# Attention beside a gated low-rank layer: the first block's order, the row tiles' slots and the second output pass's weight splits

## The chip, the cores and the metric

The kernel runs on one core of one Trainium2 chip. The metric is device time in microseconds (us). Matrix products run on TensorE (PE in the profile, with its weight loads as PEld), elementwise work on VectorE (DVE), ScalarE (ACT) and GpSimd (POOL). Transfers are issued from the queues of SyncE (SP) and of ScalarE.

## The reference

```
xn  = (x - mean) / sqrt(var + 1e-5)               # over 2048 columns, 4096 rows
q, k, v = split(xn @ Wqkv + bqkv)                 # 512 columns each
att = softmax(q @ k.T / sqrt(512)) @ v            # two sequences of 2048 rows
s   = (xn @ Wq.T) @ keys.T                        # 64 experts
g   = softmax over the 16 largest of s, 0 elsewhere
z   = (xn @ A.T) * repeat(g, 8)                   # 512 columns
y   = x + att @ Wo + bo + 2 * (z @ B.T)
```

All is fp32, with x of 2 x 2048 x 2048.

## The kernel before, in words

**Products.** Every fp32 operand is split into a high part, rounded to the format `fp32r` that TensorE takes (`split_hi`, ScalarE, L123), and the rest (`split_lo`, L126, VectorE). `product` and `multiply` issue three matmuls for one product of 128 x 128 by 128 x N: low by high, high by low, high by high (L131, and L1184 in the output stage).

**Order.** The program is written out in Python, and a scheduler orders the instructions of each engine by readiness under its own model of time, earlier code first; it also sets the semaphores. `behind(keys)` keeps the instructions of a block after the one last recorded under a key, on the same engine; it makes no engine wait for another. Rings (`Ring`, L42) hand out named slots of SBUF in turn, and a new user of a slot waits for the last one. Each engine works through its queue in order, so an instruction that waits holds up what stands behind it.

**Stages.** The 4096 rows form eight blocks of 512 rows.

1. `first_block` makes block 0 ready and computes its value columns. Four tiles of 128 rows (`rows`) are loaded from `x` (`load`), their mean and variance taken (`normal`: L196, L199, L344, L189, and POOL's power at L190), scaled (`scale`: three quarters on VectorE at L352, one on ScalarE at L356 and L357), and turned by TensorE into 16 chunks of 128 columns (`turn`, L366); each turned chunk is split into `xh`. The weights of the value columns come in eight pieces for each of two halves (`piece`, through `wv_piece` and `weights`: load at L266, splits at L123 and L126; loaded tiles `ws` have four slots, split ones `wh` eight). `mul` multiplies one group of 128 rows (one tile turned) by one piece: six matmuls of 264 columns. A group of the first half has 48 of them. `values_out` takes the sums out to `vs` and to memory.
2. Other columns of blocks 0 and 1 (`ftile`), and then blocks 2 to 7 in pairs, by sums and differences of half matrices in seven steps in place of eight (`phase`). Meanwhile the row statistics of the blocks to come are taken: `stats_steps` loads row tiles `xs` by ScalarE's queue (L214) and runs them through `row_stats` (L196). Blocks 1 to 3 take tiles of 1024 columns from three slots (`r_xs`), blocks 4 to 7 tiles of 512 columns from two (`r_xr`). One tile is loaded for each that is read, as many ahead as there are slots but one.
3. Attention: scores, softmax and the weighted sum of v.
4. Output: attention and the gated layer in one product of 1024 rows of weights, again in seven steps for eight (`STEPS`: P1, P2, P6, P5, P3, P7, P4). There are 16 units `q` of work: eight groups of rows in a first pass over half of the output columns, and the same eight in a second pass over the other half. A unit is seven steps, each of two products (t = 0, 1) of 12 matmuls.

**The output stage's queues.** A job is one step of one unit. `ahead(n)` prepares the row operand of job n, three jobs early: `load_x` at P1, then `stationary`, which forms the sums (L1133, L1135, L1136, L1138 on VectorE) and splits the step's operand into `s` (six slots, two for a job). P1's result is copied by ScalarE to `u` (L1196); P2 goes on in the same PSUM bank, so its products wait for that copy. The other results are added on VectorE (L1202, L1207, L1213; `finish`, L1173), with additions on POOL (L1209, L1214) into tiles `xo`, which `residual` loads and adds the bias to (L1168).

The output weights `wb` of a pass stay in SBUF, four slots to a step (`r_tm`). `moving(p, step, kk)` returns a load (L1096 or L1100, into `wo`) and a split for two of a step's four row chunks: 14 such units in a pass. In the last unit of the first pass (q = 7) and the first of the second, the loop's end loads and splits the second pass's weights: step m's load two steps ahead, its split when the first pass is done with that step, both units of a step together.

Of the kernel before, what the change touches and what calls it, by code (L numbers as in the profile page):

```python
# [20 lines left out]
ND = D // P  # L21
# [5 lines left out]
NT = T // P  # L27
# [36 lines left out]
def attn_ffn_kernel(ctx: ExitStack, tc, x, xT, wq, wv, wob, bqk, bv, bo, keysT, out):  # L64
# [24 lines left out]
    def half(*js):  # L89
        return Ring(sb, *(f"H{j}" for j in js))  # L90
# [111 lines left out]
    def stats_steps(i, r, cols, out):  # L202


        v, tiles = {}, {}
        per = C // cols

        def load(k):
            if k < NT * per:
                t, c = divmod(k, per)  # L210
                tiles[k] = r([P, cols], F32, "xs")
                r0 = i * T + t * P
                with behind("hi"):
                    nc.scalar.dma_start(tiles[k], x[r0 : r0 + P, c * cols : (c + 1) * cols])  # L214

        def rows(k):
            t, c = divmod(k, per)
            if k == 0:
                v["mv"] = const.tile([P, NT, 2], F32, name="mv", bufs=2)
                for n in range(len(r.tags) - 1):  # L220
                    load(n)
            if c == 0:
                v["st"] = const.tile([P, 4, 6], F32, name="st6", bufs=2)
                v["parts"] = 0
            load(k + len(r.tags) - 1)
# [96 lines left out]
    def first_block():  # L322
# [24 lines left out]
        def scale(t):  # L347
            for n in range(4):
                c, h = divmod(n, 2)
                v = rows[t][c][:, h * 512 : (h + 1) * 512]  # L350
                if n < 3:
                    last["row"] = nc.vector.tensor_scalar(  # L352
                        v, v, mv[:, t, 0:1], rs[:, t : t + 1], ALU.subtract, ALU.mult
                    )
                else:
                    nc.scalar.activation(v, v, AF.Identity, bias=nm[:, t : t + 1])  # L356
                    nc.scalar.mul(v, v, rs[:, t : t + 1])  # L357

        def turn(t, g0=0, g1=NCH // 4):
            sl = slice(t * P, (t + 1) * P)  # L360
# [15 lines left out]
        def piece(c2, h, eng=None, queue=None):  # L376
            return wv_piece(h, c2, eng, queue)
# [14 lines left out]
        for j in range(26):  # L392
            nc.tensor.matmul(pw, warm[:, :P], warm, start=True, stop=True)
        load(0, 512)
        wh = [piece(0, 0, None, nc.scalar)]
        normal(0)
        with behind("nm"):
            wh.append(piece(1, 0, None, nc.scalar))
        scale(0)
        load(1, 1024)  # L400
        turn(0, 0, 2)
        for c2 in range(2, 4):
            with behind("row"):
                wh.append(piece(c2, 0, None, nc.scalar))
        turn(0, 2, 4)
        ps = [acc() for t in range(NT)]
        for c2 in range(3):
            mul(ps[0], wh[c2], 0, c2)
        with behind("row"):
            normal(1)  # L410
        with behind("nm"):
            wh += [piece(c2, 0) for c2 in range(4, 6)]
        scale(1)
        load(2, 1024)
        for c2 in range(3, 6):
            mul(ps[0], wh[c2], 0, c2)
        turn(1)
        for c2 in range(6):
            mul(ps[1], wh[c2], 1, c2)
        with behind("row"):  # L420
            wh += [piece(c2, 0, nc.gpsimd) for c2 in range(6, N2)]
        load(3, 1024)
        constants()
        for c2 in range(6, N2):
            mul(ps[0], wh[c2], 0, c2)
            mul(ps[1], wh[c2], 1, c2)
            if c2 == 6:
                with behind("row"):
                    normal(2)
                scale(2)  # L430
                turn(2)
                with behind("row"):
                    normal(3)
        qr = router_in()
        for t in range(2):
            values_out(0, t, 0, r_ev, qr, ps[t])
        flush()
        for c2 in range(N2):
            mul(ps[2], wh[c2], 2, c2)
            if c2 == 2:  # L440
                scale(3)
                turn(3)
        for c2 in range(N2):
            mul(ps[3], wh[c2], 3, c2)
        for t in range(2, NT):
            values_out(0, t, 0, r_ev, qr, ps[t])
        flush()
        ps = [acc() for t in range(NT)]
# [443 lines left out]
        xn = nxt  # L892
    r_ph = wide(0, 1, 2, 3, 4, 5)
    r_pw = wide(8, 9, 7)
    r_xr = half(7, 8)
    r_xu = big(6, 7, 8)
    r_xv = wide(6)
    r_yv = mid(2, 3)
# [4 lines left out]
    n = 0  # L903
# [174 lines left out]
    def moving(p, step, kk):  # L1078


        small = p == 1 and STEPS.index(step) % 2 == 1

        def load():
            n = 2 * p
            if small:
                ws = tw[p, step, kk] = [r_wo1([P, T], F32, "wo") for k in range(2)]
            else:
                ws = tw[p, step, kk] = r_wo([P, 2, T], F32, "wo")
                ws = [ws[:, k, :] for k in range(2)] if step not in ("P1", "P2", "P3") else ws
# [24 lines left out]

        return load, split
# [7 lines left out]
            )  # L1123
            X[g, a, b] = t

    def stationary(q, step):


        g = q % (NB // 2 * NH)
# [6 lines left out]
            nc.vector.tensor_tensor(x[0, 0], X[g, "S1"], x[0, 0], ALU.subtract)  # L1136
        if step == "P3":
            nc.vector.tensor_tensor(x[0, 1], x[0, 1], x[0, 0], ALU.subtract)  # L1138
        src = {
            "P1": x[0, 0], "P2": x[0, 1], "P6": x[0, 0], "P5": X.get((g, "S1")),  # L1140
            "P3": x[0, 1], "P7": x[1, 0], "P4": x[1, 1],
        }[step]
        hi, lo = (r_s([P, ND, TH], FR, "s") for a in range(2))
        split_hi(hi, src)
        split_lo(lo, src, hi)
# [77 lines left out]
    def ahead(n):  # L1223

        if n >= len(jobs):
            return
        q, step = jobs[n]
        if step == "P1":
            load_x(q % NG) if q < 2 * NG else None
        stationary(q, step)  # L1230


    flush()
# [2 lines left out]
    for s in range(NSTEP + LAG):  # L1236
# [47 lines left out]
        if e in (2, 7, 12):  # L1284
            if e == 2:
                load_bo(0)
            with behind("mq"):
                ahead(e // 5)
    more = {}
    for q in range(2 * NG):  # L1290
        p = q // NG
        for t in range(NA):
# [2 lines left out]
        for n, step in enumerate(STEPS):  # L1295
# [7 lines left out]
            for t in range(NA):  # L1303
# [1 line left out]
                if step == "P1":  # L1305
                    bank[t] = ps
                combine(q, step, t, ps)
            if n + 3 + 7 * q >= 3:
                ahead(7 * q + n + 3)
            if q == NG - 1 and n == 0:  # L1310
                load_bo(1)


            m = n + 7 * q - 7 * (NG - 1)
            if 0 <= m < 7:
                with behind("act"):
                    for _, split in more.pop(m):
                        split()
            if -2 <= m < 5:
                more[m + 2] = [moving(1, STEPS[m + 2], kk) for kk in range(0, ND, 2)]  # L1320
                for load, _ in more[m + 2]:
                    load()


# [40 lines left out]
```

## Time and profile before

| | us |
|---|---|
| median of 3 runs | 2660.33 (2659.31 to 2663.43) |
| profiled execution, its own time | 2662.85 |
| its span in the profile | 2661.1 |
| TensorE busy | 2632.8 |
| VectorE busy | 1818.6 |
| ScalarE busy | 863.4 |
| POOL busy | 569.7 |
| granted TensorE clock, mean | 0.995 |

Busy time is that of an engine's instructions in this one execution; waits are what stood between them. In a line of a timeline the first number is the start in us from the beginning of the span, the second the duration, then engine, line, operation, output and inputs by the program's names, and in brackets the idle time before it with the instruction that ended it. In a list of waits come the total, the number of times and the longest. A slice's line gives each engine's busy time, the granted clock as a share of the full one, and what DMA moved.

### The profile page before, as it was taken

How to read it: one execution, taken by the hardware profiler on the slowest of the kernel's cores; microseconds unless marked ns; L12 is line 12 of the kernel's file. 1: busy time of each engine (PE TensorE's matmuls, PEld its weight loads, DVE VectorE, ACT ScalarE, POOL GpSimd, SP SyncE). 2: the span in 40 equal slices, each digit the busy share in tenths (PEclk: the TensorE clock that was granted, in tenths of full speed). 3: DMA queues.
4: the chain of work that ended last, by engine and by line, in shares of the span. 5: the costliest groups of instructions: out<-in, count | busy, mean ns of one | idle time of the engine just before them, and what ended most of it. 6: DMA issues, size and time to landing. Idle time of an engine off the chain costs nothing.

```text
span 2661.1 us, 33841 instructions
## 1 busy us (share of the span) xinstructions
PE 2632.8 (99%) x12881; PEld 2227.1 (84%) x12881; DVE 1818.6 (68%) x2493; ACT 863.4 (32%) x1285; POOL 569.7 (21%) x349
## 2 busy tenths in 40 slices
PE   7999999999999999999999999999999999989999
PEld 7889888888888888888888888888888888878887
DVE  6557849868878687756445676456667776796675
ACT  4223323333332333323233343334434222322221
POOL 1321420000000000000101111000012665565654
PEclk8999999999999999999999999999999999999999
DMA  6678885668546684536725476634467444655543
GB/s 232 222 259 278 297 283 178 211 212 296 186 147 225 230 291 137 173 125 221 286 101 191 143 269 229 206 111 143 144 205 260 167 162 159 201 188 165 178 155 107
DMA packets 243395, 530.42 MB, mean 199 GB/s; under 512 B 21608, under 2 KB 87200, under 8 KB 243232
## 3 DMA queue, kind: packets, MB, share of 16 engines
q1 hardware_dynamic: 229696, 497.29, 55.3%
q10 hardware_dynamic: 13536, 30.97, 3.4%
q8 instruction: 101, 1.65, 0.3%
q14 instruction: 62, 0.51, 0.1%
HBM read 393.80 MB, written 134.38 MB: 198 GB/s over the span
## 4 chain that ended last, share of the span: by engine, by line
PE 95%; DVE 2%; DMA 2%; issue 1%; ACT 0%; ACTq 0%; SPq 0%; DVEq 0%
PE acc L131 73%; PE acc L1184 22%; DMA xs<-in_x 1%; DVE wb L126 1%; DMA ws<-in_wv 0%; DVE st L196 0%; DVE pw L126 0%; PE acc L366 0%; DVE xq L666 0%; DMA wo<-tw_d 0%; DVE xo L1173 0%; PE misc L466 0%; PE misc L999 0%; DVE xh L126 0%; DVE wh L126 0%
## 5 line engine op out<-in xcount | busy, mean ns | idle before, releaser
L131 PE MATMUL acc<-t,pw 128*128 128x512 f32 x3024 | 695.6, 391 | 2.7 <-ACT t L123 1.8
L131 PEld LDWEIGHTS acc<-t,pw 128*128 128x128 f32 x3024 | 566.4, 188 | 121.3 <-ACT t L123 2.2
L1184 PE MATMUL acc<-wb,s 128*128 128x512 f32 x2688 | 611.8, 390 | 7.7 <-ACT u L1196 7.7
L1184 PEld LDWEIGHTS acc<-wb,s 128*128 128x128 f32 x2688 | 506.0, 188 | 113.4 <-ACT u L1196 8.2
L131 PE MATMUL acc<-ph,vt 128*128 128x512 f32 x1536 | 367.5, 390 | 0.0
L131 PE MATMUL acc<-qt,kt 128*128 128x512 f32 x1536 | 366.0, 389 | 0.0
L131 PEld LDWEIGHTS acc<-ph,vt 128*128 128x128 f32 x1536 | 287.4, 188 | 62.1 <-DVE ot L1047 1.2
L131 PEld LDWEIGHTS acc<-qt,kt 128*128 128x128 f32 x1536 | 288.2, 188 | 60.3 <-issue 0.2
L1168 POOL TENSOR_TENSOR xo<-xo,bo_bc 128x512 f32<-128x512 f32 x128 | 217.2, 1704 | 560.7 <-DMA xo<-in_x 330.2
L123 ACT CAST pw<-pw 128x1024 fp32r<-128x1024 f32 (+1 forms) x168 | 177.7, 1058 | 380.3 <-PE acc L131 225.0
L131 PE MATMUL acc<-xh,wh 128*128 128x512 f32 x1152 | 263.7, 390 | 0.0
L126 DVE TENSOR_TENSOR pw<-pw 128x1024 fp32r<-128x1024 f32 (+1 forms) x168 | 218.0, 1298 | 65.5 <-ACT pw L123 65.5
L131 PEld LDWEIGHTS acc<-xh,wh 128*128 128x128 f32 x1152 | 215.6, 188 | 45.0
L131 PEld LDWEIGHTS acc<-pw,t 128*128 128x128 f32 x2016 | 245.7, 188 | 1.5 <-DVE pw L126 0.2
L131 PE MATMUL acc<-pw,t 128*128 128x264 f32 x2016 | 246.5, 283 | 0.0
L123 ACT CAST s<-xz 128x1024 fp32r<-128x1024 f32 x112 | 118.1, 1054 | 384.6 <-PE acc L1184 312.9
L126 DVE TENSOR_TENSOR s<-xz,s 128x1024 fp32r<-128x1024 f32 x112 | 166.6, 1488 | 49.8 <-ACT s L123 49.8
L126 DVE TENSOR_TENSOR ph<-sp,ph 128x512 fp32r<-128x512 f32 x128 | 93.4, 732 | 120.3 <-ACT ph L123 119.5
L971 DVE TENSOR_TENSOR M<-M,sp 128x512 f32<-128x512 f32 x112 | 79.6, 711 | 123.5 <-ACT sp L965 123.1
L536 POOL TENSOR_TENSOR zt<-zt,g 128x512 f32<-128x512 f32 x24 | 35.0, 1467 | 494.8 <-DMA g<-gd 166.7
L126 DVE TENSOR_TENSOR wh<-wu,wh 128x512 fp32r<-128x512 f32 x96 | 96.1, 1025 | 64.9 <-ACT wh L123 64.9
L965 ACT COPY sp<-acc 128x512 f32<-128x512 f32 x128 | 74.8, 586 | 182.1 <-PE acc L131 182.0
(150 smaller groups left out, 2378.1 us busy)
## 6 DMA issues: line engine op xcount, KB each, us to landing
vt<-v_d SPq DMA_DIRECT2D x128, 512.0 KB, 3.5
pw<-sq_d SPq DMA_DIRECT2D x72, 512.0 KB, 3.5
xz<-oz_d SPq DMA_DIRECT2D x64, 512.0 KB, 4.2
xo<-in_x SPq DMA_DIRECT2D x128, 256.0 KB, 3.5
out_y<-xo SPq DMA_DIRECT2D x128, 256.0 KB, 2.5
pw<-in_wq SPq DMA_DIRECT2D x54, 512.0 KB, 3.9
wu<-in_wq SPq DMA_DIRECT2D x48, 512.0 KB, 7.6
xq<-in_xT SPq DMA_DIRECT2D x48, 512.0 KB, 6.1
```

The costliest lines, as they stand in the source:

```text
L123: return nc.scalar.copy(hi, src)
L126: return (eng or nc.vector).tensor_tensor(lo, src, raw(hi), ALU.subtract)
L131: last["pe"] = nc.tensor.matmul(ps, st(a_), mv(b_), start=first and n == 0, stop=end and n == 2)
L536: nc.gpsimd.tensor_tensor(zt, zt, gx[n], ALU.mult)
L965: nc.scalar.copy(st, ps)
L971: nc.vector.tensor_tensor(M[blk], M[blk], st, ALU.max)
L1168: nc.gpsimd.tensor_tensor(xs, xs, bo_bc[q // (NB // 2 * NH), c], ALU.add)
L1184: nc.tensor.matmul(ps, st[a_][:, kk, sl], mv[b_], start=not more and kk == 0 and n == 0, stop=kk == ND - 1 and n == 2, skip_group_check=more,)
```

## The change

Three places are rewritten.

In `first_block`, tile 0 is loaded, normalised and scaled first. The weights' pieces follow in groups (`pieces(n)`), all loaded by SP's queue, with splits ordered after the latest scaling of a tile (a new key, `mul`, on ScalarE's last scaling) and all on ScalarE and VectorE. The four groups are multiplied one after the other, each by all eight pieces; the next tile is normalised, scaled and turned within the loop. Before, groups 0 and 1 shared the loop over the pieces, and pieces 6 and 7 had their low part on POOL.

In `stats_steps`, row tiles are loaded ahead by the number of slots less two, and `r_xr` has a third slot, H6.

In the output stage, `stationary` is cut into `sums` and `split`; the operand of P6 is split together with that of P5, one step later, but for q = 0. The second pass's 14 weight units are handled one by one: a list `at` gives the step, counted from the start of unit 7, at which each load and split is issued, over twelve steps for the splits.

```diff
-                for n in range(len(r.tags) - 1):
+                for n in range(len(r.tags) - 2):
                     load(n)
...
-            load(k + len(r.tags) - 1)
+            load(k + len(r.tags) - 2)
...
-                    nc.scalar.mul(v, v, rs[:, t : t + 1])
+                    last["mul"] = nc.scalar.mul(v, v, rs[:, t : t + 1])
...
         load(0, 512)
-        wh = [piece(0, 0, None, nc.scalar)]
         normal(0)
-        with behind("nm"):
-            wh.append(piece(1, 0, None, nc.scalar))
         scale(0)
+        wh = []
+        def pieces(n):
+            with behind("row", "nm", "mul"):
+                while len(wh) < n:
+                    wh.append(piece(len(wh), 0))
+        turn(0, 0, 2)
+        pieces(2)
+        turn(0, 2, 4)
+        pieces(4)
         load(1, 1024)
-        turn(0, 0, 2)
-        for c2 in range(2, 4):
-            with behind("row"):
-                wh.append(piece(c2, 0, None, nc.scalar))
-        turn(0, 2, 4)
         ps = [acc() for t in range(NT)]
...
-        with behind("row"):
-            wh += [piece(c2, 0, nc.gpsimd) for c2 in range(6, N2)]
...
+        for t in range(NT):
+            if t + 1 < NT:
+                with behind("row"):
+                    normal(t + 1)
+            if t == 0:
+                pieces(6)
+                load(2, 1024)
+            for c2 in range(N2):
+                if t + 1 < NT and c2 == 2:
+                    scale(t + 1)
+                if t == 0 and c2 == 4:
+                    pieces(N2)
+                    load(3, 1024)
+                    constants()
+                if t + 1 < NT and c2 == 6:
+                    with behind("pe"):
+                        turn(t + 1)
+                mul(ps[t], wh[c2], t, c2)
...
-    r_xr = half(7, 8)
+    r_xr = half(6, 7, 8)
...
-        small = p == 1 and STEPS.index(step) % 2 == 1
+        small = p == 1 and (2 * STEPS.index(step) + kk // 2) % 4 > 1
...
-        stationary(q, step)
+        sums(q, step)
+        if step != "P6" or q == 0:
+            if step == "P5" and q:
+                split(q, "P6")
+            split(q, step)
...
-    more = {}
+    more = [moving(1, step, kk) for step in STEPS for kk in range(0, ND, 2)]
+    at = [-3, -2, -1, 0, 1, 2, 2, 3, 4, 5, 6, 7, 7, 8, 9, 10, 11]
...
-            m = n + 7 * q - 7 * (NG - 1)
-            if 0 <= m < 7:
-                with behind("act"):
-                    for _, split in more.pop(m):
-                        split()
-            if -2 <= m < 5:
-                more[m + 2] = [moving(1, STEPS[m + 2], kk) for kk in range(0, ND, 2)]
-                for load, _ in more[m + 2]:
-                    load()
+            while at and at[0] <= n + 7 * q - 7 * (NG - 1):
+                at.pop(0)
+                k = 14 - len(at)
+                if k > 0:
+                    with behind("act"):
+                        more[k - 1][1]()
+                if k < 12:
+                    more[k + 2][0]()
```

The new rule for `small` picks the same units as the old one (kk is 0 or 2), and the changed test before `load_x` always held.

More of the change, by code (lines that the diff above doesn't have):

```diff
@@ L394, in first_block @@
         load(0, 512)
-        wh = [piece(0, 0, None, nc.scalar)]
         normal(0)
-        with behind("nm"):
-            wh.append(piece(1, 0, None, nc.scalar))
         scale(0)
-        load(1, 1024)
-        turn(0, 0, 2)
-        for c2 in range(2, 4):
-            with behind("row"):
-                wh.append(piece(c2, 0, None, nc.scalar))
-        turn(0, 2, 4)
-        ps = [acc() for t in range(NT)]
-        for c2 in range(3):
-            mul(ps[0], wh[c2], 0, c2)
-        with behind("row"):
-            normal(1)
@@ L411, in first_block @@
[L411 to L420, printed above, removed]
-            wh += [piece(c2, 0, nc.gpsimd) for c2 in range(6, N2)]
[L422 to L427, printed above, removed]
-                with behind("row"):
[L429 to L433, printed above, removed]
@@ L434, in first_block @@
-        qr = router_in()
[L435 to L445, printed above, removed]
+        wh = []
[3 more added lines that the diff above has]
+                    wh.append(piece(len(wh), 0))
@@ L446, in first_block @@
+        qr = router_in()
+        for t in range(NT):
             values_out(0, t, 0, r_ev, qr, ps[t])
@@ L1124, in load_x, with sums @@
             X[g, a, b] = t
-    def stationary(q, step):
+    def sums(q, step):
         g = q % (NB // 2 * NH)
@@ L1138, in stationary, with split @@
             nc.vector.tensor_tensor(x[0, 1], x[0, 1], x[0, 0], ALU.subtract)
+    def split(q, step):
+        g = q % (NB // 2 * NH)
         src = {
-            "P1": x[0, 0], "P2": x[0, 1], "P6": x[0, 0], "P5": X.get((g, "S1")),
-            "P3": x[0, 1], "P7": x[1, 0], "P4": x[1, 1],
-        }[step]
+            "P1": (0, 0), "P2": (0, 1), "P6": (0, 0), "P3": (0, 1), "P7": (1, 0), "P4": (1, 1),
+        }.get(step)
+        src = X[(g, *src)] if src else X[g, "S1"]
         hi, lo = (r_s([P, ND, TH], FR, "s") for a in range(2))
@@ L1228, in ahead @@
         if step == "P1":
-            load_x(q % NG) if q < 2 * NG else None
-        stationary(q, step)
+            load_x(q % NG)
+        sums(q, step)
[3 more added lines that the diff above has]
+            split(q, step)
     flush()
@@ L1307, in attn_ffn_kernel @@
                 combine(q, step, t, ps)
-            if n + 3 + 7 * q >= 3:
-                ahead(7 * q + n + 3)
+            ahead(7 * q + n + 3)
             if q == NG - 1 and n == 0:
                 load_bo(1)
-            m = n + 7 * q - 7 * (NG - 1)
-            if 0 <= m < 7:
-                with behind("act"):
-                    for _, split in more.pop(m):
-                        split()
-            if -2 <= m < 5:
-                more[m + 2] = [moving(1, STEPS[m + 2], kk) for kk in range(0, ND, 2)]
-                for load, _ in more[m + 2]:
-                    load()
+            while at and at[0] <= n + 7 * q - 7 * (NG - 1):
[6 more added lines that the diff above has]
+                    more[k + 2][0]()
 def kernel(**inputs):
```

## The prediction

> **What bounds the kernel now.** I read the page's busy shares first, then everything that TensorE waited for, then each place of a long wait in order of time.
>
> ```profile
> PE 2632.8 (99%) x12881; PEld 2227.1 (84%) x12881; DVE 1818.6 (68%) x2493; ACT 863.4 (32%) x1285; POOL 569.7 (21%) x349
> ```
>
> TensorE is busy for 2632.8 of 2661.1 us, and the change keeps all matrix products. So only the 28.3 us of idle, and time at a lower clock, can be won. The waits of TensorE over the whole span (line, releaser, total, times, longest):
>
> ```profile
> PE acc L1184 <- ACT u L1196: 7.7, 1, 7.7
> PE acc L366 <- DVE xs L352: 5.1, 1, 5.1
> PE acc L131 <- DVE wh L126: 4.6, 1, 4.6
> PE acc L366 <- issue: 2.4, 1, 2.4
> PE acc L131 <- ACT t L123: 1.8, 1, 1.8
> ...
> PE acc L131 <- DVE t L126: 0.9, 1, 0.9
> PE acc L131 <- ACT wh L123: 0.5, 1, 0.5
> ```
>
> The rest is 1.2 us at the start and 4.0 us after the last product. The second, third and fourth lie in the first 50 us; the first is at 2350 us; the last three at 531 and 238 us. First the opening, from the timelines of TensorE, VectorE and ScalarE (start, duration):
>
> ```profile
> 9.72 0.63 ACT L123 CAST wh<-ws 128x528 fp32r<-128x528 f32 x1 [2.84 <-DMA ws<-in_wv]
> 12.32 0.71 DVE L126 TENSOR_TENSOR wh<-ws,wh 128x528 fp32r<-128x528 f32 x1 [1.24 <-ACT wh L123]
> 12.95 1.46 DVE L352 TENSOR_SCALAR xs<-xs,mv,rs 128x512 f32<-128x512 f32 x3
> 13.55 3.67 PE L366 MATMUL acc<-ident,xs 128*128 128x128 f32 x16 [5.13 <-DVE xs L352]
> 25.67 2.79 PE L131 MATMUL acc<-wh,xh 128*128 128x264 f32 x11 [4.64 <-DVE wh L126]
> 49.00 1.96 PE L366 MATMUL acc<-ident,xs 128*128 128x128 f32 x16 [2.36 <-issue]
> ```
>
> VectorE has the statistics of tile 0 at 7.3 us and POOL the power at 8.0, but scaling (L352) starts at 12.95: two weight subtractions stand ahead of it, and they wait for weights. The second place is the border of the output's two passes (ScalarE, VectorE, TensorE):
>
> ```profile
> 2345.19 0.58 ACT L1196 COPY u<-acc 128x512 f32<-128x512 f32 x1
> 2355.36 1.21 DVE L1136 TENSOR_TENSOR xz<-xz 128x1024 f32<-128x1024 f32 x1
> 2356.66 1.05 ACT L123 CAST s<-xz 128x1024 fp32r<-128x1024 f32 x1 [10.89 <-DVE xz L1136]
> 2357.61 0.58 ACT L1196 COPY u<-acc 128x512 f32<-128x512 f32 x1
> 2358.24 62.00 PE L1184 MATMUL acc<-wb,s 128*128 128x512 f32 x263 [7.74 <-ACT u L1196]
> ```
>
> ScalarE stands in its queue before the split of P6's operand, which waits for VectorE's sum L1136; the second `u` copy is behind it, and TensorE needs that copy. VectorE is late because it is full: its busy time is 8.69, 10.00, 10.00, 10.00 and 10.00 us in the 10 us slices from 2310 to 2360. The copies of neighbouring units start exactly 38.08 us apart; over this border (2309.74 to 2396.02, two units) it is 86.28, so it costs 86.28 - 76.16 = 10.1 us: 7.7 of idle and 2.4 of slow clock.
>
> [...] 0.50 granted from 25 to 30 us after the 4.64 us wait, 0.63 from 2350 to 2360. [...] ScalarE and VectorE run strictly in queue order; the 10.89 us above show it. [...] the 128x1024 subtraction into `s` takes 1.21 us at least and 2.24 at most.
>
> **The change, part by part.**
>
> *Opening.* The weights' eight pieces leave ScalarE's DMA queue for SP's, behind tile 0's two SP loads; their splits are ordered behind the scaling of tile 0, and no longer go to POOL (2.56 us for two there become 1.31 on VectorE). Groups 0 to 3 each run over all eight pieces in turn. In the built order TensorE has 36 products, transposes, 60, transposes, 48, transposes, 48 of group 3; before 36, 58, 50, 48. Nothing is added or taken away there, so what counts is when VectorE delivers.
> Arrival: in 1.5 us slices DMA moved 2.3 MB by 9.0 us before. Tile 0 (1.05 MB) and four pieces (4 x 0.27) are now first in the queues, 2.1 MB, so I take the fourth piece to land near 9 us (estimate; it was 15.5). On SP the four issues, 0.33 to 0.46 us each, are past at about 3.5 us; tile 1's loads follow when tile 0 has landed (4.2, as the third piece's issue did before) and are in by 11 us at 3.1 MB, wanted at 15.4: covered by 4 us. SP then issues tile 2 and half of tile 3; pieces 4 and 5 wait behind these and for a freed slot (12 us), about 4.7 MB in, which was moved at 15 us; landed by 17.
> VectorE: scaling 8.0 to 9.5. Then, from about 9.9 (ScalarE casts one piece, 0.63, then the first transposes): low parts of tile 0, 2 x 1.67 = 3.34; eight weight subtractions, 4 x 1.31 = 5.24; statistics of tile 1, 2.46; its small operations 0.43; its scaling 1.46. Sum 12.93, so the last weight piece is ready at 22.8 and pieces 4 and 5, wanted at 18.4, are there. TensorE: group 0 ends at 22.8 + 0.7 = 23.5. A group is 48 products at 0.121 us (165 in the 20 us from 240), 5.8: group 1 ends at 29.3, and 1 us for slow clock makes it 30.3. Tile 2 is scaled by then: 22.8 + low parts 3.3 + statistics 2.5 + `vs`, small ones and POOL's power 1.4 + scaling 1.5 = 31.5. Transposes end at 32.5, group 2 at 38.3. From there to group 3 the chain is the one of before (its `vs`, L344, power, scaling, transposes): 46.65 to 50.82 = 4.2 us. Group 3 starts at 42.5, with 0.3 for clock 42.8. Before 50.82: **8.0 us less**. Ends: 4 less if the clock stays low for all of group 1 (5.8 more there, 1.8 of it hidden by scaling), 11 less if there is no slow clock and the two gaps of VectorE I counted vanish.
>
> *Rows' slots.* `stats_steps` loads one row tile ahead and not two; in the last four blocks there are three slots and not two. 88 loads on ScalarE's queue stay 88. ScalarE no longer waits for VectorE to free the slot just read (up to 4.9 us at L214). This bears on the 531 us wait (2.7) and the 238 us one (0.5). I take half: **1.5 less**. Ends: 4 less (with the 0.96 clock there), 3 more if the later loads keep VectorE waiting. The cover is TensorE's lead in split weights; the rival below prices its loss.
>
> *Second pass split over twelve products.* `moving(1, ...)` is loaded and split in 14 single units over 12 products (q = 7, P1 to q = 8, P3) and not in seven pairs over seven; loads start one product earlier. The splits are the same. Their VectorE cost before was 27.6 us (all `wb` subtractions, 2312 to 2359), with 38.08 - 26.7 = 11.4 us free per unit (28 of 40 us busy elsewhere). In the built VectorE order the sums of q = 8 and its L1136 now stand ahead of the splits for P3, P7 and P4, which took 13.3 us (1.72 + 1.21 + 5.78 + 2.28 + 2.28). So L1136 falls from 2355.4 to about 2341.5, and P6's low part from 2362.1 to 2348.8; TensorE wants it at 2309.7 + 8 x 5.44 = 2353.2. ScalarE's P6 cast is then done at 2343.4, the `u` copies follow their products, and the wait is gone: **10.1 us less**. Later splits: P3's end near 2355 and are wanted at 2364; P4's near 2365, wanted at 2375. P6's split is also issued one step later in the code; in steady state the built order on ScalarE and VectorE is that of before, so I cost it at nothing. Its cover is VectorE's 4.4 us; beyond it each late us is a TensorE us. Low end of this part: 5 less.
>
> Sum: 8.0 + 1.5 + 10.1 = 19.6. Profiled execution 2662.85 (span 2661.1, 1.75 around it) becomes 2643.3; the median of the runs shown, 2660.33, becomes 2640.7, so **2641**.
>
> **Rivals.**
> - *The border's wait moves.* P6's low part or P1's split stays late, for the backlog of eight units (8 x 1.97 = 15.8 us into 9.8 free) is 6 us. For it: POOL is busy 30.5 of these 50 us and slows subtractions. Against: the order above leaves 4 us. A 4 us wait and 1 of clock: 2646.
> - *The opening gains half.* Weights land late or group 1 runs slow: [...] Then 4 less: 2645. With the first rival 2651.
> - *Slower: row tiles starve VectorE.* Between 60 and 300 us 24 tiles of 128x1024 take 5.3 us (median) to land, and one ahead may mean waiting for each. VectorE has 240 - 161.7 = 78.3 us free there. If each waits fully, 24 x 5.3 = 127 us, 49 too many: 2641 + 49 = 2690. It decides from 4.3 us per tile ((78.3 + 24.6) / 24, the bound of slower below). Against: the first of each pair is loaded a tile earlier; 12 x 5.3 = 64 us fits; today's waits there are 11.0.
>
> **How the numbers follow.** Likeliest 0.66, own range 2637 to 2645; border 0.12; opening 0.09; starved rows 0.07; other mixtures 0.06, split between no change (0.05) and slower (0.01). A difference under 0.2% (5.3 us) can't be told from none here. Faster 0.66 + 0.12 + 0.09 = 0.87, same 0.05, slower 0.08. The range runs from all favourable ends (11 + 4 + 10.1: 2635) to both small rivals together (2651), one more for run to run: 2652.
>
> **What would show it.** Right: scaling of tile 0 begins near 8 us; group 3's products near 43; no wait of TensorE at L1196's successor, copies 38.08 us apart across the border; the waits at 531 shorter. Wrong: transposes still wait over 3 us at 9; a new wait behind `s` or `wb` after 2330; idle after `xs` loads on VectorE far over today's 49.8 us in total with TensorE waiting for `wh`.

## The result, and the profile after

| | before | after |
|---|---|---|
| median of 5 runs of each, us | 2661.26 | 2643.41 (2639.48 to 2644.76) |
| ratio | | **0.9929** [0.9915, 0.9944] |
| profiled execution, its own time, us | 2662.85 | 2641.34 |
| its span, us | 2661.1 | 2639.6 |
| granted TensorE clock, mean | 0.995 | 1.000 |
| group 3's products start, us | 50.82 | 42.65 |
| from there to the second `u` copy of the first output unit, us | 1992.75 | 1989.44 |
| second `u` copies of q = 7 and q = 9 apart, us | 86.28 | 76.16 |

The prediction was 2641, its own range 2637 to 2645. The median is 17.85 us lower than before (0.67%); the means of the five are 18.8 us apart, and that is the 0.71% of the ratio. The last three rows are the places of the three edits, one after the other: 8.17 + 3.31 + 10.12 = 21.6 us, all of the 21.5 us between the two profiled executions. That this is 3.7 us more than between the medians is taken up with the clock, below. Of all executions in this document one, of `open_only`, took 11266.45 us, and its row leaves it out. Line numbers are each kernel's own: L1136 and L1196 before are L1121 and L1184 now.

The page's busy times of the changed kernel:

```profile
PE 2624.7 (99%) x12881; PEld 2220.4 (84%) x12881; DVE 1822.3 (69%) x2495; ACT 863.6 (33%) x1285; POOL 571.8 (22%) x347
```

TensorE does the same 12881 matmuls in 8.1 us less busy time. No work was taken away, so this is work done at a higher clock: the kernel before has 27.3 us with 0.50 granted up to its last product (13.65 in the opening, 3.4 at 533 us, 10.2 at the border), the changed one none. Idle time fell from 28.3 to 14.9 us, and 13.4 + 8.1 make the 21.5. Everything that TensorE waited for in the changed kernel:

```profile
PE acc L131 <- DVE wh L126: 5.0, 3, 2.2
PE acc L366 <- issue: 2.4, 1, 2.4
PE acc L131 <- DVE yv L746: 1.8, 1, 1.8
PE misc L393 <- DVE warm L390: 1.2, 1, 1.2
PE acc L131 <- ACT wh L123: 0.5, 1, 0.5
```

Gone are the wait for the `u` copy at the border (7.7 us), the one for tile 0's scaling (5.1) and both for `t` near 531 us (1.8 and 0.9). The one for `wh` at 238 us (0.5) stays, at 230 us now. The wait for weights stays at 5.0 us, but in three pieces of at most 2.2 where it was one of 4.6. One wait is new: 1.8 us behind `yv`. The opening, from the timelines of VectorE and TensorE:

```profile
8.14 1.46 DVE L352 TENSOR_SCALAR xs<-xs,mv,rs 128x512 f32<-128x512 f32 x3 [0.76 <-POOL rs L190]
...
21.42 1.32 DVE L126 TENSOR_TENSOR wh<-ws,wh 128x528 fp32r<-128x528 f32 x2
```
```profile
8.74 2.01 PE L366 MATMUL acc<-ident,xs 128*128 128x128 f32 x16
...
19.57 1.61 PE L131 MATMUL acc<-wh,xh 128*128 128x264 f32 x11 [2.22 <-DVE wh L126]
21.02 1.91 PE L366 MATMUL acc<-ident,xs 128*128 128x128 f32 x16
22.69 7.55 PE L131 MATMUL acc<-wh,xh 128*128 128x264 f32 x60
30.29 2.01 PE L366 MATMUL acc<-ident,xs 128*128 128x128 f32 x16
32.37 6.10 PE L131 MATMUL acc<-wh,xh 128*128 128x264 f32 x48
40.83 2.00 PE L366 MATMUL acc<-ident,xs 128*128 128x128 f32 x16 [2.36 <-issue]
```

Scaling starts at 8.14, as soon as POOL's power is there, and TensorE goes over to the transposes without a wait: the 26 matmuls on a constant tile at its start (L393, not changed) end there too, near 8.9. VectorE ends the eighth piece at 22.74, where the prediction had 22.8. The border (ScalarE, then VectorE):

```profile
2331.03 1.06 ACT L123 CAST s<-xz 128x1024 fp32r<-128x1024 f32 x1 [4.43 <-PE acc L1172]
...
2336.42 0.59 ACT L1184 COPY u<-acc 128x512 f32<-128x512 f32 x1 [2.08 <-PE acc L1172]
...
2374.50 0.59 ACT L1184 COPY u<-acc 128x512 f32<-128x512 f32 x1 [2.08 <-PE acc L1172]
```
```profile
2329.54 1.21 DVE L1121 TENSOR_TENSOR xz<-xz 128x1024 f32<-128x1024 f32 x1
...
2337.10 3.94 DVE L126 TENSOR_TENSOR s<-xz,s 128x1024 fp32r<-128x1024 f32 x2
```

The second copy of each unit comes 38.08 us after the last one and waits for its product. P6's cast (2331.03) still stands in front of both copies, but it no longer waits for VectorE. P6's sum (L1121, before L1136) is done at 2330.75, and its low part, the first of the two at 2337.10, near 2339.1; TensorE wants it 5.44 us after P1's last product, 2336.42 + 5.44 = 2341.9.

### The profile page after: what moved, and what is told of

Its sections match the earlier page's. It is cut to its first block, busy times and chain, and to the rows that moved or that the text cites. A ratio compares the mean times of both kernels' runs of the same rounds, so it can differ in the third digit from the quotient of the medians.

```text
span 2639.6 us, 33827 instructions
## 1 busy us (share of the span) xinstructions
PE 2624.7 (99%) x12881; PEld 2220.4 (84%) x12881; DVE 1822.3 (69%) x2495; ACT 863.6 (33%) x1285; POOL 571.8 (22%) x347
## 4 chain that ended last, share of the span: by engine, by line
PE 98%; DVE 1%; DMA 0%; ACT 0%; issue 0%; SPq 0%; ACTq 0%; DVEq 0%
PE acc L131 75%; PE acc L1172 23%; DMA xs<-in_x 0%; DVE st L196 0%; PE acc L366 0%; DVE xh L126 0%; PE misc L451 0%; PE misc L984 0%; DVE wh L126 0%; DMA v_d<-vs 0%; PE misc L1024 0%; PE misc L1025 0%; PE misc L481 0%; ACT xh L123 0%; ACT xs L357 0%
## 5 line engine op out<-in xcount | busy, mean ns | idle before, releaser
L126 DVE TENSOR_TENSOR s<-xz,s 128x1024 fp32r<-128x1024 f32 x112 | 173.2, 1548 | 42.0 <-ACT s L123 42.0
```

Of the source, the lines that this page charges most:

```text
L126: return (eng or nc.vector).tensor_tensor(lo, src, raw(hi), ALU.subtract)
```

## The experiments

Twelve kernels: the edits alone and in part together, their finer parts, and extra work that uses up a cover (the time by which an operand may come later before TensorE waits). The kernel before was timed again beside them, with medians of 2662.12 us for the first four rows, 2661.47 for the next four and 2660.44 for the last four. So kernels are compared by their ratios. Beside the time the table has the three places of the table above, from each kernel's profile; "middle" is the time from group 3's start to the first output unit's second `u` copy.

| kernel | median us | ratio to before, 95% | group 3 starts | middle | border |
|---|---|---|---|---|---|
| `open_only`: the opening's edit alone | 2654.91 | 0.9970 [0.9959, 0.9982] | 45.23 | 1989.63 | 86.71 |
| `second_only`: the output stage's edit alone | 2651.12 | 0.9955 [0.9943, 0.9967] | 49.69 | 1992.75 | 76.16 |
| `rows_only`: the rows' slots alone | 2657.87 | 0.9985 [0.9979, 0.9992] | 49.68 | 1988.87 | 86.02 |
| `no_rows`: all but the rows' slots | 2644.30 | 0.9931 [0.9919, 0.9943] | 45.52 | 1991.33 | 76.16 |
| `spread_only`: the 14 single units alone | 2652.15 | 0.9966 [0.9952, 0.9980] | 50.67 | 1989.20 | 76.16 |
| `p6_only`: P6's later split alone | 2660.44 | 0.9997 [0.9989, 1.0006] | 49.75 | 1992.33 | 85.52 |
| `slots_only`: the third slot, loads two ahead | 2657.48 | 0.9982 [0.9975, 0.9989] | 50.92 | 1987.61 | 85.08 |
| `scale_first`: scaling ahead of the weights' splits | 2660.35 | 0.9995 [0.9986, 1.0003] | 49.78 | 1992.28 | 85.27 |
| `late_weights`: changed, four pieces on ScalarE's queue | 2643.98 | 0.9937 [0.9922, 0.9952] | 45.62 | 1989.71 | 76.16 |
| `cover_2`: changed, two operations more | 2645.98 | 0.9945 [0.9930, 0.9960] | 45.19 | 1988.72 | 80.51 |
| `cover_8`: changed, eight operations more | 2656.75 | 0.9986 [0.9979, 0.9992] | 44.35 | 1988.95 | 90.44 |
| `best`: changed, row tiles two ahead and value columns out later | 2639.96 | 0.9922 [0.9907, 0.9937] | 43.97 | 1987.57 | 76.16 |

### The three edits one at a time

```diff
 # open_only: first_block of the changed kernel in the kernel before
 # second_only: sums/split, `at` and the loop of single units in the kernel before
 # rows_only
-                for n in range(len(r.tags) - 1):
+                for n in range(len(r.tags) - 2):
...
-            load(k + len(r.tags) - 1)
+            load(k + len(r.tags) - 2)
...
-    r_xr = half(7, 8)
+    r_xr = half(6, 7, 8)
 # no_rows: the changed kernel without the three lines of rows_only (and with the old
 # rule for `small`, which picks the same units)
```

> The kernel before with the new first block alone. Theory (three separate gains): group 3's products start near 42.7 us in place of 50.8, TensorE's wait at the border of the two passes stays at 7.7 and the one at 531 stays; 8.2 us less, ratio 0.9969. Rival (the opening's gain is partly taken back by the stages behind it, whose weights are loaded by the same queues): group 3 as early, but less than 5 us in the whole, with new waits of TensorE before 300 us.

> The kernel before with the output's second pass split over twelve products and P6's operand split one step later, nothing else. Theory: copies of u 38.08 us apart across the border, 10.1 us less, ratio 0.9962, opening as before. Rival (the border's wait depends on what the earlier stages leave in the queues): some of the 7.7 us stays, 5 us less.

> The kernel before with the row tiles' two edits alone. Theory: the wait at 531 us (2.7, with its slow clock) goes and one near 880 us behind a row load on VectorE comes (1.8): 3 us less at most, ratio 0.999 to 1.000. Rival (the edits are worth nothing in the whole, since a wait gone is one come): 0.0 plus or minus 1.5 us.

> The changed kernel without the row tiles' edits. Theory: 8.2 + 10.1 = 18.3 us less than before, ratio 0.9931, with the wait at 531 back and none near 880. Rival (the row edits are what keeps VectorE free in the changed kernel): under 15 us less.

Each edit moved its own column. Of the others, group 3's start and the border stay near the kernel before (within 1.2 and 0.5 us), but the middle does not: `open_only`, without the rows' edit, is 3.1 us shorter there. So `open_only` met the 8.2 us expected of it partly by luck: its group 3 starts at 45.23 and not near 42.7, which is 5.6 us, and the rest comes from the middle. The new waits before 300 us that its rival asked for are not there. The gains alone are 0.30, 0.45 and 0.15%, 0.90% together; all three at once give 0.71%. The difference of 0.19 is inside what the intervals leave open (the root of their squared half-widths is 0.23), so no overlap between the edits is shown. `rows_only`, 4 us by its ratio, is a little beyond the 3 us that it was given at most. The output stage's edit gives the most. With the opening alone, the border keeps its full wait (the waits of TensorE in `open_only`):

```profile
PE acc L1169 <- ACT u L1181: 8.0, 1, 8.0
```

and the same place in `second_only`, with an untouched opening, shows both copies waiting for their products alone (ScalarE's timeline):

```profile
2344.08 0.59 ACT L1199 COPY u<-acc 128x512 f32<-128x512 f32 x1 [1.68 <-PE acc L1187]
2346.75 0.59 ACT L1199 COPY u<-acc 128x512 f32<-128x512 f32 x1 [2.08 <-PE acc L1187]
```

The rows' slots are the least certain by time: beside the other two they are worth 0.02%, 0.5 us, which is nothing that these intervals can tell. The middle column is sharper. The five profiles with the rows' edit as changed (the changed kernel, `rows_only`, `late_weights`, `cover_2`, `cover_8`) have 1988.72 to 1989.71, mean 1989.14; the seven without (the kernel before and six of the table) 1989.20 to 1992.75, mean 1991.47. That is 2.3 us. The kernels without the edit vary because the wait at 531 us does: five of the seven wait there for ScalarE's `t` (1.3 to 1.9 us), `open_only` and `spread_only` do not, and theirs are the two shortest middles, no longer than with the edit. None of the seven profiles with a third slot (`slots_only` and `best` included) has that wait. Going by these profiles, the edit keeps that wait from coming, and the old slots do so only in some executions.

### What in the output stage's edit does it

```diff
 # spread_only: the kernel before, with the loop of single units
+    more = [moving(1, step, kk) for step in STEPS for kk in range(0, ND, 2)]
+    at = [-3, -2, -1, 0, 1, 2, 2, 3, 4, 5, 6, 7, 7, 8, 9, 10, 11]
 # p6_only: the kernel before, with sums/split and
+        if step != "P6" or q == 0:
+            if step == "P5" and q:
+                split(q, "P6")
+            split(q, step)
```

> The kernel before with the second pass's weights over twelve products, P6's operand split as before. Theory: all of the border's gain, 10.1 us less. Rival (both edits are needed): at most half of it.

> The kernel before with P6's operand split one step later in the code, the second pass's weights as before. Theory (VectorE's load binds at the border, and the scheduler puts the split where it was): the border's wait stays at 7.7 us, no change, within 1 us. Rival (the place of P6's cast ahead of the second u copy is the cause): the wait goes or halves, 5 to 10 us less.

The spread gives the whole 10.1 us of the border. P6's later split gives no measurable difference, and the wait stands as before (waits of TensorE in `p6_only`, then ScalarE's timeline):

```profile
PE acc L1187 <- ACT u L1199: 6.9, 1, 6.9
```
```profile
2354.52 1.04 ACT L123 CAST s<-xz 128x1024 fp32r<-128x1024 f32 x1 [10.06 <-DVE xz L1136]
2355.47 0.58 ACT L1199 COPY u<-acc 128x512 f32<-128x512 f32 x1
```

The cast still stands ahead of the second copy and still waits for VectorE's sum, now 10.06 us where it was 10.89. So the cause is VectorE's backlog of paired weight splits ahead of L1136, as the prediction had it, and not the place of P6's split; `cover_2`, next, brings the wait back by VectorE's load alone. The 6.9 us say nothing against it: the six profiles with the weights in pairs, this one included, have 6.3 to 8.0 at this place.

### How much cover the border has left

P6's sum is put off by VectorE operations that change nothing (eight of them in `cover_8`):

```diff
             nc.vector.tensor_tensor(x[1, 0], x[0, 0], x[1, 0], ALU.subtract)
+            for _ in range(2 if q == 8 else 0):
+                nc.vector.tensor_tensor(x[0, 0], x[0, 0], x[0, 0], ALU.max)
```

> The changed kernel with two added VectorE operations (a maximum of a tile with itself, 128x1024, 1.2 to 2.2 us each) ahead of P6's sum of q = 8; values do not change. In the built order of ScalarE, P6's cast stands ahead of both u copies. Theory, the queue's order: the sum, which ended at 2330.75, now ends 2.4 to 4.4 us later, plus the splits in between, near 2334 to 2337.5, and the cast then takes 1.1; the first u copy, which started at 2336.42, is late by 0.5 to 2 us, TensorE waits up to 2.7 us for it at P2 with ScalarE's copy u as releaser, and the time is 1 to 4 us above that of the changed kernel. Rival, only VectorE's slack counts (2.8 us before P6's product in the profile of the changed kernel): no wait of TensorE over 1 us at the border, the time within 1 us of the changed kernel's, 2642.5 to 2644.5.

> The same with eight added operations. In the built order of ScalarE, both u copies now stand ahead of P6's cast. Theory, the prediction's cover of P6's split: its low part, ready at 2339.1 in the changed kernel, comes 9.7 to 15 us later, 2349 to 2354; TensorE wants it at 2341.9, so it waits 7 to 12 us with VectorE's s as releaser, and the second u copies of q = 7 and q = 9 stand 83 to 90 us apart in place of 76.16; the time is 8 to 13 us above that of the changed kernel. Rival, the cover is much more than the slack read from the profile (the planner moves other splits behind): a wait under 4 us and the time at most 4 us more.

In `cover_2` the copies are behind the cast again (ScalarE's and TensorE's timelines):

```profile
2338.91 1.04 ACT L123 CAST s<-xz 128x1024 fp32r<-128x1024 f32 x1 [10.65 <-DVE xz L1123]
2339.86 1.07 ACT L1186 COPY u<-acc 128x512 f32<-128x512 f32 x2
```
```profile
2340.49 15.74 PE L1174 MATMUL acc<-wb,s 128*128 128x512 f32 x61 [2.44 <-ACT u L1186]
```

The sum ended at 2338.79, which is later than the 2334 to 2337.5 expected, as more of VectorE's other work came ahead of it, and 8.0 us later than in the changed kernel; TensorE was 1.6 later there by its own (P1's last product at 2338.0 for 2336.4), so 6.4 us of delay became 2.44 us of wait: the cover is 4.0 us. In `cover_8` the scheduler put both copies ahead of the cast, and the wait is for the operand itself:

```profile
2354.00 46.25 PE L1174 MATMUL acc<-wb,s 128*128 128x512 f32 x192 [11.55 <-DVE s L126]
```

The added operations took 15.7 us (3.45 + 3.95 + 8.32 in VectorE's timeline), 11.55 of them came out as a wait: 4.2 us of cover. P6's low part ended near 2353.9, which is 14.2 us later once TensorE's own 0.6 us at this place is taken off; so 2.8 of the 4.2 us are the slack that the changed profile shows (2341.9 less 2339.1), and the other 1.4 is VectorE work ahead of the low part that the scheduler put behind it. The border grew by 4.4 and 14.3 us, more than the waits by 1.9 and 2.7 us; the granted clock was low after them, 0.66 from 2340 to 2345 us in `cover_2` and 0.57 from 2355 to 2360 in `cover_8`. Both theories of a cover hold here, one after the other: through ScalarE's queue for a short delay, through P6's operand for a long one. The wait of 11.55 us is within the 7 to 12 expected; the border's 90.44 us and the loss (0.57% by the ratios, 15 us) are a little over the upper ends.

### What in the rows' slots does it

```diff
 # slots_only: the kernel before, wide tiles two ahead as before, narrow ones now too
-    r_xr = half(7, 8)
+    r_xr = half(6, 7, 8)
```

> The kernel before with a third slot for the tiles of 512 columns alone, so these are loaded two ahead, and the tiles of 1024 columns two ahead as before. Theory (a third slot frees ScalarE, one ahead makes VectorE wait): the wait at 531 is shorter than 2.7 and there is none near 880; 1 to 4 us less, and VectorE waits under 43 us in total for row tiles. Rival (two ahead with three slots blocks ScalarE behind VectorE again): the wait at 531 stays; 0 us.

The third slot for the narrow tiles gives what `rows_only` gives, 0.18% against 0.15%, with loads two ahead. VectorE's idle time for row tiles is 32.3 us (49.8 before, 39.0 in `rows_only`, 42.9 in the changed kernel), and the middle is 1987.61 us, 1.5 less than the 1989.14 of the kernels that load one ahead. `best`, two ahead with three slots as well, has 32.8 and 1987.57; the five that load one ahead have 37.6 to 42.9 and at least 1988.72. So the slot is enough for the gain, and by these profiles loading fewer tiles ahead takes some of it back. By the times the two can't be told apart. The wait at the border is 1.4 us shorter here (6.3), for reasons not followed up.

### What in the opening does it

```diff
 # scale_first: the kernel before, with tile 0's scaling and transposes ahead of the splits
+        early = []
+        for c2 in range(4):
+            ch, cc = divmod(2 * c2, HC)
+            early.append(r_ws([P, 2, VH], F32, "ws"))
+            nc.scalar.dma_start(early[c2], wv[0, ch, :, cc : cc + 2, :])
...
         normal(0)
         scale(0)
         load(1, 1024)
         turn(0, 0, 2)
+        split_early(2)
         turn(0, 2, 4)
+        split_early(4)
 # late_weights: the changed kernel, its first four pieces loaded by `early` as above
```

> The kernel before, with only this changed in the first block: the splits of the first four weight pieces stand behind tile 0's scaling on VectorE and ScalarE; their loads stay on ScalarE's queue beside tile 1's and 2's, groups 0 and 1 still share the pieces, pieces 6 and 7 still have their low part on POOL. Theory (the order on VectorE is what held tile 0 back): scaling near 8.1 us in place of 12.95, most of the opening's gain, 5 to 7 us of 8.2, the rest missing because pieces land as late as 15.5. Rival (the late weights bind, so the queue is what matters): scaling early, but TensorE waits for pieces instead; under 3 us.

> The changed kernel, but the first four pieces of the weights are loaded by ScalarE's queue from the start, as before, so that tile 1's loads go out on the other queue at the same time [...]; order of scaling, splits, groups and engines as in the changed kernel. Theory, landing order counts: casts of the four pieces near 10.2, 12.2, 14.1 and 16.1 us (8.8, 10.7, 12.5 and 13.2 in the changed kernel), VectorE done with the eighth piece 1.5 to 3 us after 22.74, group 3 starts 1.5 to 3 us after 42.65 with full clock (44 to 46), up to 48 with a slow clock; the time is 1.5 to 4 us above that of the changed kernel. Rival, the order on VectorE and the groups' order give the whole gain: group 3 at 42.6 to 44 and the time within 1 us of the changed kernel's.

`scale_first` was expected to gain 5 to 7 us; no gain shows (0.9995 [0.9986, 1.0003]), which is the size that its rival had. Scaling did start at 8.12 and tile 0's transposes at 8.86, and TensorE ended the first 36 products at 23.9 instead of 28.5. Then tile 1's scaling came late (VectorE's and POOL's timelines):

```profile
23.91 2.43 DVE L352 TENSOR_SCALAR xs<-xs,mv,rs 128x512 f32<-128x512 f32 x3 [2.29 <-POOL rs L190]
```
```profile
22.04 1.32 POOL L126 TENSOR_TENSOR wh<-ws,wh 128x528 fp32r<-128x528 f32 x1 [13.80 <-DMA ws<-in_wv]
23.32 0.56 POOL L190 TENSOR_TENSOR rs<-ve,nhalf 128x1 f32<-128x1 f32 x1
```

VectorE had tile 1's statistics ready for POOL at 20.4, but POOL's power stands behind a weight split that POOL still does here, and that split waited until 22.04 for its weights. So late weights have a part in it, as the rival said, here by way of POOL's queue. Of the 4.6 us won, 1.0 is left at group 3 against the kernel before. Some of this loss is the clock of this one execution: tile 3's transposes start at 46.52 (49.00 before), but take 3.51 us with 0.50 granted from 47 to 49 us (1.96 before, at 1.00). So tile 0's scaling was the first link of the opening, and not the only one; the next that the trace shows is POOL's split ahead of the power. The changed kernel takes it away, and it also no longer lets groups 0 and 1 share the pieces; which of the two counts more was not tried.

`late_weights` is not decided by its time: 0.6 us above the changed kernel by the medians, 0.08% (2 us) by the ratios, with intervals that overlap. The profile is plainer. The fourth piece was cast at 15.60 (in the changed kernel by 13.2), and VectorE ended the eighth at 23.74, 1.0 us later and not the 1.5 to 3 expected. But that 1.0 us is not the queue's. TensorE's 26 matmuls at the start, which stand ahead of the transposes in its queue, took 8.69 us in this profile and 7.69 in the changed kernel's, so the first transposes came at 9.71 and not at 8.74. From there to the end of the eighth piece it is 14.03 us, and 13.94 to 14.00 in the changed kernel, `open_only`, `no_rows`, `cover_2`, `cover_8` and `best`, whose weights come by SP's queue. So the weights' queue is worth at most 0.1 us on this chain, and the gain is that of the orders and of POOL's split: VectorE takes the weights after tile 0's low parts anyway.

### A version against two of the remaining waits

```diff
+        ahead_ = 2
...
-                for n in range(len(r.tags) - 2):
+                for n in range(ahead_):
...
-            load(k + len(r.tags) - 2)
+            load(k + ahead_)
...
         for t in range(NT):
-            values_out(0, t, 0, r_ev, qr, ps[t])
+            with behind("row"):
+                values_out(0, t, 0, r_ev, qr, ps[t])
```

> The changed kernel with two edits: row tiles are again loaded two ahead (of both widths, with three slots each), and the first half's value columns are taken out of PSUM behind the statistics recorded last. Theory: the 1.76 us wait at 876 us behind a late row tile goes, VectorE's idle time for row tiles falls from 42.9 us to 30 to 40, and the 2.36 us wait ahead of group 3 goes or halves; the time is 2 to 5 us below that of the changed kernel, 2638.5 to 2641.5. Rival: both waits move to the next late operand, and the time is within 1 us of the changed kernel's, 2642.5 to 2644.5.

The wait behind `yv` is gone (it is in `cover_2` and `cover_8` too, with one tile ahead), and the 2.36 us one ahead of group 3 has become 1.0 and 0.5 us. TensorE's waits in `best`:

```profile
PE acc L131 <- DVE wh L126: 5.1, 3, 2.4
PE misc L394 <- DVE warm L391: 1.2, 1, 1.2
PE acc L367 <- DVE xs L353: 1.0, 1, 1.0
PE acc L131 <- DVE xh L126: 0.9, 2, 0.5
PE acc L131 <- ACT wh L123: 0.5, 1, 0.5
```

VectorE's idle time for row tiles falls from 42.9 to 32.8 us, and the middle is 1987.57, the shortest of all. The ratio of 0.9922 is 0.07% under the changed kernel's, with overlapping intervals: the places moved as the theory said, but a lower time is not shown.

## Why the prediction was right, point by point

**The second pass, 10.1 us: right by its mechanism.** Copies 38.08 us apart, border 76.16, 10.12 us less; `spread_only` alone does it. The times by which it got there: L1136's start was put at 2341.5, and TensorE reached the border 11.4 us earlier (2298.34 for 2309.74), so at 2330.1 in the changed profile; it is at 2329.54. P6's low part, 2337.4 in the same way, came near 2339.1, so that the slack was 2.8 us and not 4.4. As a cover for added work it was 4.0 to 4.2, for the reasons above, and a short delay reached TensorE through the `u` copies, which the prediction's price for P6's edit had not named. One reading there is short: the longest subtraction into `s` was 2.33 us in the kernel before, not 2.24; no term rests on it. Of the 112, the 35 that ran while POOL was idle took 1.21 to 1.23 us; the 46 that had POOL busy for over nine tenths of their time took 1.21 to 2.33, 1.70 in the median. And the 10.89 us show the order of ScalarE's queue; that of VectorE's shows in its idle 1.24 us before the weight subtraction at 12.32, with the scaling behind it, whose last input was there from 8.0 on.

**P6's edit at nothing: right.** `p6_only` is 0.9997 [0.9989, 1.0006].

**The rows' slots, 1.5 us: right in sign, undersized if anything.** The middle column says 2.3; alone the edit gives 0.15% (4 us), in company nothing measurable. Of the two waits that it was to bear on, the one at 531 us went and the one at 238 us stayed. The slower rival, starved rows, did not come: VectorE waited 42.9 us for row tiles instead of 49.8. A small one of its kind did (VectorE's timeline and TensorE's, changed kernel):

```profile
873.64 0.69 DVE L196 BATCH_NORM_STATS2 st<-xs 128x6 f32<-128x512 f32 x1 [3.39 <-DMA xs<-in_x]
874.25 1.21 DVE L126 TENSOR_TENSOR t<-xq,t 128x1024 fp32r<-128x1024 f32 x1
875.37 1.44 DVE L746 TENSOR_TENSOR yv<-xv,acc 128x264 f32<-128x264 f32 x4
```
```profile
875.85 10.81 PE L131 MATMUL acc<-pw,t 128*128 128x264 f32 x87 [1.76 <-DVE yv L746]
```

A row tile is late by 3.39 us, VectorE's queue stands, and TensorE waits for `yv` behind it. The same tile is late by 2.64 us in `late_weights` and 2.48 in `rows_only`, with 1.0 and 0.9 us of wait, and by 1.47 and 1.31 in `cover_8` and `cover_2`, with none: about 1.6 us of lateness is covered. `slots_only` and `best`, with two tiles ahead, have no such wait.

**The opening, 8.0 us: met in the profile, too high on average; the mis-sized term is the slow clock.** In the profiled execution each link stands near where it was put: eighth piece 22.74 (22.8), group 1 done at 22.69 + 7.55 = 30.24 (30.3), group 2 at 38.47 (38.3), group 3 at 42.65 (42.8). For group 1 this is luck: group 0 ended near 24.2 for 23.5, because its last 12 products stand behind tile 1's transposes in TensorE's order, and the "1 us for slow clock" that was to bring group 1 to 30.3 did not come in at all. In the other four profiles with this opening (`open_only`, `no_rows`, `cover_2`, `cover_8`) slow clock did come in (0.50 granted for 6.84, 6.80, 6.82 and 3.42 us between 10 and 50), and group 3 starts at 45.23, 45.52, 45.19 and 44.35. Six profiles with the old opening have 49.68 to 50.92, mean 50.26; five with the new one, the changed kernel's own included, 42.65 to 45.52, mean 44.59. The gain is 5.7 us on average, within the prediction's ends of 4 and 11.

Where the other 2.3 us went can be read off. From the first transposes to group 3 it is 33.91 us in the changed kernel's profile and 35.97, 35.91, 35.95 and 35.56 in the other four, so by this estimate slow clock costs 1.55 us on average over the five. The prediction's sum carries 0.3 for it: its 1 us ahead of group 1's end is hidden behind tile 2's scaling. Another 0.4 us is what the prediction doesn't have: TensorE's 26 first matmuls take 7.19 to 8.58 us in these five profiles, and where they are long, the transposes start up to 0.9 us later than in the changed kernel's (8.74 to 9.61). Why their time varies is open. And 0.56 us is the starting point, 50.82, which is that much above the mean of the old opening. With 2.3 and 10.1 the 5.7 us make 18.1, and the record has 17.85 (medians) to 18.8 (means): the sum of 19.6 was too high by 0.8 to 1.8.

## What to carry to other kernels

At the border ScalarE's cast waited 10.89 us for VectorE's sum, the `u` copy behind it in the queue waited with it, and TensorE waited 7.74 us for the copy. So the copy paid for VectorE's backlog: thinning the backlog (about one unit per step, not two) gave the 10.1 us, where splitting the late operand one step later gave nothing. The cover of an operand is measured by adding work until a wait shows; the slack read off one profile was 2.8 us here, the cover 4.0 to 4.2. Before pricing the removal of one wait on a chain, list what releases the next link: scaling tile 0 first alone moved TensorE 4.6 us ahead and gave no gain that shows, since the power for tile 1 stood behind POOL's split. And before a difference of 1 us between two profiles is put down to an edit, find where it begins: in `late_weights` it was there ahead of the edited part.

## What the runs showed of the hardware

In these profiles the granted clock falls to 0.50 in spells, and each profile's time at 0.50 between 10 and 50 us is a whole multiple of 3.41 us, to within 0.03. In 1 us slices of `open_only` (busy time of TensorE, granted clock, DMA share, GB/s):

```profile
19.00:20.00 1.00, 0.00 (x0) 0.91 0.74 233
20.00:21.00 1.00, 0.97 (x4) 0.50 0.11 18
21.00:22.00 1.00, 1.00 (x7) 0.50 0.85 226
22.00:23.00 1.00, 1.00 (x6) 0.50 0.84 315
23.00:24.00 1.00, 1.00 (x10) 0.88 0.52 77
```

The clock is halved from 19.82 (0.18 us of the first slice at 0.50 give its 0.91) to 23.24: 3.42 us. Summed over 10 to 50 us, the time at half clock is 13.66 us in the kernel before, 6.84, 6.80, 6.82 and 3.42 in `open_only`, `no_rows`, `cover_2` and `cover_8`, and 0 in the changed kernel's profile: 4, 2, 2, 2, 1 and no spells of 3.41 us. The second spell of `open_only` starts at 43.72, 23.90 us after the first, and 23.90 is 7 times 3.414.

What starts a spell is not shown. Before the first one of `open_only` TensorE had idle gaps of 1.70, 1.03 and 0.50 us after 10 us, and one of 1.67 in which the clock fell. But the changed kernel's profile has gaps of 1.71, 1.03 and 2.22 us at this place, and no spell. In the two full slices at 0.50 above in which TensorE is busy throughout, it began 7 and 6 matmuls, and 10 to 11 in those from 24 to 34 us, at 1.00. By estimate from the 3.41 us and the 0.50, a spell costs 1.7 us of work when TensorE is busy through it.

The difference of 3.7 us between the profiled pair and the medians fits this: the profiled execution of the changed kernel is 2.07 us below its median, that of the kernel before 1.59 above its own. The five executions of the changed kernel have mean clocks of 1.000 (2641.34 and 2639.48 us), 0.999 (2643.41) and 0.998 (2644.76 and 2644.40), and the profiled one is of the first kind. What decides between them is not shown by a run.
